# Projecting three units of the third batch's context between the ranking of the tokens and the first expert

## The chip, the cores and the metric

The kernel runs on one core of one Trainium2 chip. The metric is the device time of one launch in microseconds (us), of which a profiled execution also leaves a trace of every engine and DMA. Engines are named as in the profile: PE is TensorE (PEld its weight loads), DVE is VectorE, ACT is ScalarE, POOL is GpSimd and SP is SyncE, which here only issues DMAs. A lower time is better.

## The reference

Two layers act on x (8 batches, 100 tokens, 512 features) in fp32. Each layer has an attention and a mixture of eight experts, of which every token uses two.

```python
x = x + L0_xattn(layernorm(x), ctx, q_w, q_b, k_w, k_b, v_w, v_b, o_w, o_b)   # causal: only ctx[:, :100] counts
x = x + L0_ffn(layernorm(x), gamma, beta, Wg, bg, W1, b1, W2, b2)             # 8 experts, gelu, 2048 wide
x = x + L1_xattn(layernorm(x), ctx, ln_g, ln_b, Wq, Wkv, Wm, Wo, bo)          # keys: own 100 + projected ctx 722
x = x + L1_ffn(x, w_router, w_gate, w_up, w_down, ln_gamma, ln_beta)          # 8 experts, silu, 1024 wide

# the part of L1_xattn that the change is about: one projection serves as keys and as values
mem = split_heads(ctx @ Wm)          # (8, 722, 512) @ (512, 1024), 16 heads of 64
k = concatenate([k, mem]); v = concatenate([v, mem])
out = softmax(q k^T / 8) v
```

The expert part routes each token to the two experts with the largest router logits and adds the two answers by their normalized weights.

## The kernel before

**Stages.** The first attention runs over 32 units (4 groups of heads by 8 batches). Its output projection and the router follow, tile by tile over seven tiles of 128 tokens. When a group of tiles has its logits, `Route.group` (from L236) finds each token's two experts, ranks the tokens of each expert with two matmuls (L252, L253), and POOL sends the token rows into a table in DRAM, `sent`, by indirect DMA (L267). After the last group, `Route.order` sorts the experts by load, and each expert then fetches its rows (`arrived`, L344), transposes them into columns (L157, gain and shift on DVE at L164), computes its hidden layer (L680, Gelu on ACT at L684) and its products (L356). A second attention and a second expert part follow.

**Units of the second attention.** It runs over 64 units (b, ic): batch b, and a pair of heads ic of 8. A plain unit projects the context: for each of two halves of 361 columns, four matmuls (each of which the profile counts twice) and one eviction by ACT (L425, L429, `context_columns`); then six transposes and their evictions turn the result into values (L437 to L442, `context_rows`). Scores, softmax, transposes of the probabilities and the weighted sums follow.

**Kept units.** For the units in `EARLY` the projection is made before, by `project_early`, and stored in the DRAM tables `kept_keys` and `kept_values` (L457, L447). In the second attention such a unit loads both instead of computing them, and the first half of the next unit's projection is put beside it. Five units each of batches 0 and 1 are kept. Batch 0's are projected during the last units of the first attention and during the output projection, batch 1's between the first expert part and the second attention. Batches below `len(EARLY)` also spread the sums of their softmax by a POOL copy and a PE transpose (L792, L822), the others by three small DMAs through DRAM (L795, L797).

**The weights' ring.** `Weights` holds eight buffers of 1 MB. `load` takes the next pieces in a fixed order; a piece takes the buffer that comes free, and its DMA is issued on SP. Before, the eight first pieces are the four matrices of the first attention, two of `Wm`, and the two halves of batch 0's context; the experts' weights follow. The first two pieces of the first expert are loaded in `Route.order`, the next six when its first rows have arrived (a one-element POOL copy at L56 ties each to them).

**What sets the order.** The program is written in the order of the code, and a scheduler then places each engine's instructions; each engine's queue runs in that order. SP's queue holds at this place: the two fills of the DRAM tables with zeros, the stores of kept units, eight register loads of the experts' order (L297), and the weights.

Of the kernel before, what the change touches and what calls it, by code (L numbers as in the profile page):

```python
# [8 lines left out]
F32 = mybir.dt.float32  # L9
AF = mybir.ActivationFunctionType  # L10
ALU = mybir.AluOpType
AX = mybir.AxisListType

P = 128
D = 512
DC = D // P
B, T, S = 8, 100, 722
NT = B * T
HALF = NT // 2
NTILE = -(-NT // P)  # L20
# [10 lines left out]

EARLY = ((0, 1, 3, 5, 7), (0, 1, 3, 5, 7))
KEPT = {u: k for k, u in enumerate((b, ic) for b in range(len(EARLY)) for ic in EARLY[b])}

# [32 lines left out]
def two_layers(ctx: ExitStack, tc: tile.TileContext, a: dict, out: bass.AP):  # L67
# [9 lines left out]
    def context(b, h):  # L77
        return a["ctxT"][:, b, h * (S // 2) : (h + 1) * (S // 2)].rearrange("(c p) s -> p c s", p=P)

    pieces = [a[n] for n in ("k_w", "q_w", "v_w", "o_w")]  # L80
    W_EARLY = len(pieces)
    pieces += [a["Wm"][g] for g in range(2)] + [context(0, h) for h in range(2)]
    W_L0F = len(pieces)
    owner = [None, None]
# [120 lines left out]
    class Route:  # L205
# [29 lines left out]

        def group(self, i0, i1, xn):  # L236

# [10 lines left out]
            for i in range(i0, i1):  # L248
                nc.vector.tensor_tensor(self.before[:, i + 1, :], self.before[:, i, :], self.sel[:, i, :], ALU.add)
            ps = self.psum.tile([P, NTILE + 1, NE], F32, tag=self.tag, name=f"ps_rank{self.layer}")  # L250
            more = int(i1 == NTILE)
# [218 lines left out]
    with tc.tile_pool(name="a0", bufs=1) as ap, tc.tile_pool(name="a0w", bufs=3) as aw, tc.tile_pool(  # L470
# [24 lines left out]

        fill(sent)
        weights.load(W_L0F)
        fill(answers)

# [67 lines left out]
        for part in range(2):  # L567
            columns(0, part)
        units = [(c, b) for c in range(DC) for b in range(B)]
        prs, prTs = {}, {}  # L570
        steps = project_early(
            0, weights.tiles[W_EARLY + 2 : W_L0F], weights.tiles[W_EARLY : W_EARLY + 2], lambda: (
                fp.tile([P, S], F32, tag="nil", name="mT0", bufs=2), fp.tile([P, NSC, P], F32, tag="mv", name="mv0", bufs=2)
            ), ps, ("tp", "av"), lambda k: nc.sync.dma_start,
        )
        for n in range(len(units) + 2):
# [31 lines left out]
        def logits0(i):  # L608
            xT = xTf[:, :, i * P : i * P + rows[i]]
            to_columns(xT, xl[:, i, :], 0, rows[i], ps)  # L610
            router_logits(route.logits, i, xT, wg0, bg0, ps, "av")
            for i0, i1 in GROUPS[0]:
                if i1 == i + 1:
                    route.group(i0, i1, lambda i: xl[:, i, :])

# [17 lines left out]

        route.order(lambda: weights.load(W_L0F + 2))
        for _ in steps:
            pass
        where, more, (m1, m2) = route.where, route.more, route.m
# [433 lines left out]
```

## Time and profile before

| what | value |
|---|---|
| median of 3 runs | 1884.36 us (1884.31 to 1885.33) |
| the profiled execution | 1883.63 us, of it the span from first to last instruction 1882.0 us |
| mean granted PE clock | 0.959 |
| PE busy | 1725.5 us (92% of the span), 10414 matmuls |
| PEld busy | 1306.4 us |
| DVE, ACT, POOL busy | 594.9, 479.7, 147.8 us |
| DMA | 227.87 MB, mean 121 GB/s |
| all context projections (L425) | 1024 matmuls, 80 of them with the context in the weights' ring |

The span starts at the first instruction, and all places in time are counted from there. The page divides the span into 40 slices of 47 us and gives each engine's busy share in tenths. The timeline lists instructions in order with their start, duration and what ended the idle time before them; an answer by stretches gives busy time, granted clock and DMA share of chosen intervals. A busy PE is not always a PE at its peak, and a halved clock lengthens its matmuls.

### The profile page before, as it was taken

How to read it: one execution, taken by the hardware profiler on the slowest of the kernel's cores; microseconds unless marked ns; L12 is line 12 of the kernel's file. 1: busy time of each engine (PE TensorE's matmuls, PEld its weight loads, DVE VectorE, ACT ScalarE, POOL GpSimd, SP SyncE). 2: the span in 40 equal slices, each digit the busy share in tenths (PEclk: the TensorE clock that was granted, in tenths of full speed). 3: DMA queues.
4: the chain of work that ended last, by engine and by line, in shares of the span. 5: the costliest groups of instructions: out<-in, count | busy, mean ns of one | idle time of the engine just before them, and what ended most of it. 6: DMA issues, size and time to landing. Idle time of an engine off the chain costs nothing. (4 is left out here: it accounts for less than half of the span.)

```text
span 1882.0 us, 26422 instructions
## 1 busy us (share of the span) xinstructions
PE 1725.5 (92%) x10414; PEld 1306.4 (69%) x10414; DVE 594.9 (32%) x1462; ACT 479.7 (25%) x1400; POOL 147.8 (8%) x237
## 2 busy tenths in 40 slices
PE   5999689999999879999999999999999849999990
PEld 2455479999999645666666666666666528999990
DVE  4464510011111220454344424444444331111115
ACT  2364211111111132333333323333333210010110
POOL 4010310000000220000000000000000030000003
PEclk9999889999999989999999999999999969999995
DMA  9901374465555361131020300202201145555523
GB/s 367 414 28 56 124 284 169 182 222 189 203 201 219 108 235 45 40 96 56 5 37 5 59 3 5 37 6 37 27 6 15 6 159 221 192 185 200 207 79 114
DMA packets 74657, 227.87 MB, mean 121 GB/s; under 512 B 26273, under 2 KB 37161, under 8 KB 58129
## 3 DMA queue, kind: packets, MB, share of 16 engines
q1 hardware_dynamic: 53020, 177.98, 27.7%
q0 software_dynamic: 9888, 30.06, 5.1%
q10 hardware_dynamic: 11604, 17.95, 3.2%
q8 instruction: 86, 1.41, 0.3%
q14 instruction: 59, 0.48, 0.1%
HBM read 177.12 MB, written 48.83 MB: 120 GB/s over the span
## 5 line engine op out<-in xcount | busy, mean ns | idle before, releaser
L425 PE MATMUL ps_m<-cb,w 128*128 128x361 f32 x944 | 315.7, 486 | 0.0
L356 PE MATMUL ps_y<-h,w 128*128 128x256 f32 (+7 forms) x1536 | 280.5, 344 | 0.0
L356 PEld LDWEIGHTS ps_y<-h,w 128*128 128x128 f32 x1536 | 268.6, 190 | 7.9
L425 PEld LDWEIGHTS ps_m<-cb,w 128*128 128x128 f32 x944 | 180.5, 196 | 110.5 <-issue 18.0
L680 PE MATMUL ps_h<-xgT,w 128*128 128x256 f32 (+7 forms) x1024 | 189.5, 346 | 0.0
L680 PEld LDWEIGHTS ps_h<-xgT,w 128*128 128x128 f32 x1024 | 180.8, 192 | 5.8
L784 ACT ACTIVATE pr<-ps_sc,m 100x822 f32<-100x822 f32 x128 | 119.9, 942 | 175.7 <-issue 89.9
L808 DVE COPY prT<-ps_ptA 128x500 f32<-128x500 f32 x128 | 82.1, 678 | 187.1 <-PE ps_ptA L807 187.1
L782 DVE TENSOR_REDUCE m<-ps_sc 100x1 f32<-100x822 f32 x128 | 123.8, 1009 | 46.7 <-PE ps_sc L778 46.7
L684 ACT ACTIVATE h<-ps_h,s_b 128x256 f32<-128x256 f32 (+7 forms) x128 | 56.1, 438 | 303.8 <-PE ps_h L680 303.8
L429 ACT COPY mT<-ps_m 128x361 f32<-128x361 f32 x128 | 58.8, 460 | 251.5 <-PE ps_m L425 226.1
L414 PE MATMUL ps_col<-xT,w 128*128 128x400 f32 x320 | 115.1, 518 | 1.3 <-ACT xT L166 1.3
L950 PE MATMUL ps_g<-xgT,w 128*128 128x256 f32 (+7 forms) x512 | 104.3, 347 | 0.0
L950 PE MATMUL ps_u<-xgT,w 128*128 128x256 f32 (+7 forms) x512 | 102.8, 344 | 0.0
L414 PEld LDWEIGHTS ps_col<-xT,w 128*128 128x128 f32 x320 | 61.9, 197 | 47.3 <-issue 4.2
L950 PEld LDWEIGHTS ps_g<-xgT,w 128*128 128x128 f32 x512 | 91.4, 192 | 3.0
L950 PEld LDWEIGHTS ps_u<-xgT,w 128*128 128x128 f32 x512 | 90.7, 190 | 2.7
L778 PE MATMUL ps_sc<-mT,qT 64*100 64x311 f32 (+1 forms) x512 | 91.3, 468 | 0.0
L828 PEld LDWEIGHTS ps_av<-prT,mv 128*64 128x64 f32 (+1 forms) x1536 | 67.9, 137 | 31.3 <-issue 28.9
L955 ACT ACTIVATE sg<-ps_g 128x256 f32<-128x256 f32 (+7 forms) x64 | 22.3, 348 | 238.8 <-PE ps_g L950 238.8
L828 PE MATMUL ps_av<-prT,mv 128*64 128x100 f32 (+1 forms) x1536 | 80.6, 253 | 0.0
L807 PEld LDWEIGHTS ps_ptA<-ident,pr 100*128 100x128 f32 x640 | 65.2, 141 | 20.7 <-issue 10.6
(242 smaller groups left out, 1799.6 us busy)
## 6 DMA issues: line engine op xcount, KB each, us to landing
w<-in_W SPq DMA_DIRECT2D x64, 1024.0 KB
w<-in_w_gate SPq DMA_DIRECT2D x16, 1024.0 KB
w<-in_w_up SPq DMA_DIRECT2D x16, 1024.0 KB
w<-in_w_down SPq DMA_DIRECT2D x16, 1024.0 KB
sent<-nil SPq DMA_DIRECT2D x25, 512.0 KB
answers<-nil SPq DMA_DIRECT2D x25, 512.0 KB
cb<-in_ctxT ACTq DMA_DIRECT2D x16, 722.0 KB
xg<-sent POOLq DMA_DIRECT2D x18, 256.0 KB
```

The lines of the kernel that those rows point to most:

```text
L356: nc.tensor.matmul(py[:, k, :n], ws[f // 4][:, f % 4, dc * P : (dc + 1) * P], h[:, f, :n], start=f == 0, stop=f == nf - 1,)
L414: nc.tensor.matmul(ps[:, :HALF], w[c // 4][:, dc, (c % 4) * P : (c % 4 + 1) * P], xT[:, dc, cols], start=dc == 0, stop=dc == DC - 1,)
L425: nc.tensor.matmul(pm[:, : S // 2], w_m[ic // 4][:, dc, (ic % 4) * P : (ic % 4 + 1) * P], cb[h][:, dc, : S // 2], start=dc == 0, stop=dc = ...
L429: nc.scalar.copy(mT[:, h * (S // 2) : (h + 1) * (S // 2)], pm[:, : S // 2])
L680: nc.tensor.matmul(ph[:, :n], w[:, dc, j * P : (j + 1) * P], xg[:, dc, :n], start=dc == 0, stop=dc == DC - 1,)
L778: nc.tensor.matmul(sc[:, bank, c0:c1], qT[r, ic, q0 : q0 + T], keys_, start=True, stop=True)
L782: nc.vector.tensor_reduce(m, sc[:, :, :NKH], AX.XY, ALU.max, negate=True)
L784: nc.scalar.activation(pr.rearrange("p (a n) -> p a n", a=2), sc[:, :, :NKH], AF.Exp, bias=m, accum_out=sums[:, j : j + 1],)
L807: nc.tensor.transpose(pt[:, c, :], pr[:, T + c * P : T + (c + 1) * P], ident[:T, :T])
L808: nc.vector.tensor_copy(prT[:, : NSC - 1, :], pt)
L828: nc.tensor.matmul(po[r, 0, :], vj, prT[j][:w, c, :], start=c == 0, stop=c == NSC)
L950: nc.tensor.matmul(p_[:, :n], w_[:, dc, j * P : (j + 1) * P], xg[:, dc, :n], start=dc == 0, stop=dc == DC - 1,)
```

## The change

Three units of batch 2, with ic 1, 4 and 7, join the kept ones. Their context comes as two more pieces of the weights' ring, after the fill of the second DRAM table, in buffers that the first attention's matrices leave. Their projection is written after the ranking of the last group of tokens, before the first expert. To hold it there, `group` gets the two context tiles for its last call and adds to one element of each a zero that depends on the group's selection. With a third entry in `EARLY`, batch 2 spreads its softmax sums by the transpose.

```diff
-EARLY = ((0, 1, 3, 5, 7), (0, 1, 3, 5, 7))
+EARLY = ((0, 1, 3, 5, 7), (0, 1, 3, 5, 7), (1, 4, 7))
...
     pieces += [a["Wm"][g] for g in range(2)] + [context(0, h) for h in range(2)]
+    W_LATE = len(pieces)
+    pieces += [context(2, h) for h in range(2)]
     W_L0F = len(pieces)
...
-        def group(self, i0, i1, xn):
+        def group(self, i0, i1, xn, held=()):
...
+            for t in held:
+                nc.vector.scalar_tensor_tensor(
+                    t[:1, 0, :1], self.sel[:1, i1 - 1, :1], 0.0, t[:1, 0, :1], ALU.mult, ALU.add
+                )
             ps = self.psum.tile([P, NTILE + 1, NE], F32, tag=self.tag, name=f"ps_rank{self.layer}")
...
         fill(sent)
-        weights.load(W_L0F)
+        weights.load(W_LATE)
         fill(answers)
+        weights.load(W_L0F)
...
-        steps = project_early(
-            0, weights.tiles[W_EARLY + 2 : W_L0F], weights.tiles[W_EARLY : W_EARLY + 2], lambda: (
-                fp.tile([P, S], F32, tag="nil", name="mT0", bufs=2), fp.tile([P, NSC, P], F32, tag="mv", name="mv0", bufs=2)
-            ), ps, ("tp", "av"), lambda k: nc.sync.dma_start,
-        )
+        def kept_tiles():
+            mT = fp.tile([P, S], F32, tag="nil", name="mT0", bufs=2)
+            return mT, fp.tile([P, NSC, P], F32, tag="mv", name="mv0", bufs=2)
+
+        def by_sync(k):
+            return nc.sync.dma_start
+
+        early, late = weights.tiles[W_EARLY + 2 : W_LATE], weights.tiles[W_LATE:W_L0F]
+        steps = project_early(0, early, weights.tiles[W_EARLY : W_EARLY + 2], kept_tiles, ps, ("tp", "av"), by_sync)
...
-                    route.group(i0, i1, lambda i: xl[:, i, :])
+                    route.group(i0, i1, lambda i: xl[:, i, :], late if i1 == NTILE else ())
...
         route.order(lambda: weights.load(W_L0F + 2))
         for _ in steps:
             pass
+        for _ in project_early(2, late, weights.tiles[W_EARLY : W_EARLY + 2], kept_tiles, ps, ("tp", "av"), by_sync):
+            pass
```

More of the change, by code (lines that the diff above doesn't have):

```diff
@@ L496, in two_layers @@
         fill(sent)
+        weights.load(W_LATE)
+        fill(answers)
         weights.load(W_L0F)
-        fill(answers)
         xT = columns_tile("xT0")
```

## The prediction

> **What bounds the kernel now.** I read the page first. TensorE is busy for 92% of the span, so what matters is where it is not, and where its clock is low. The slices show two such places in the middle of the kernel; the change touches the first, slices 4 and 5 (188 to 282 us), and the long stretch from slice 16 on, the second attention.
>
> ```profile
> PE   5999689999999879999999999999999849999990
> PEclk9999889999999989999999999999999969999995
> ```
>
> Next the timeline of the first place, where the last group of rows is ranked, the rows are sent to DRAM and the first expert begins:
>
> ```profile
> 223.85 0.62 PE L252 MATMUL ps_rank<-before,every 128*128 128x24 f32 x2 [3.19 <-DVE sel L247]
> ...
> 236.78 1.18 POOL L344 DMA_DIRECT2D xg<-sent  x2 [5.39 <-issue]
> ...
> 239.83 1.94 PE L157 MATMUL ps_tp<-ident,xg 128*128 128x128 f32 x8 [14.94 <-DMA xg<-sent]
> ...
> 243.08 5.70 PE L680 MATMUL ps_h<-xgT,w 128*128 128x256 f32 x16
> 246.78 1.28 ACT L684 ACT_TABLE_LOAD   x1 [23.74 <-PE ps_h L680]
> ...
> 248.83 13.34 PE L680 MATMUL ps_h<-xgT,w 128*128 128x256 f32 x61
> ```
>
> TensorE does nothing for 14.94 us, between the last ranking matmul and the arrival of the expert's rows. The first two blocks of the expert's hidden layer then take 5.7 us. From the third on a block takes 1.73 us (the distance of its Gelus), so two take 3.46. The answer by stretches says why, with TensorE's busy time, the granted clock and the DMA share in each row:
>
> ```profile
> 219.98:223.39 3.41, 0.68 (x10) 0.50 0.42 161
> ...
> 240.46:243.87 3.41, 2.80 (x12) 0.50 0.82 280
> 243.87:247.29 3.42, 3.42 (x9) 0.50 0.89 335
> 247.29:250.70 3.41, 3.41 (x18) 1.00 1.05 381
> ```
>
> The clock is halved from 216.57 to 247.29 us. A stretch of 2.80 of 3.41 us busy didn't bring it back, a full one did; elsewhere 3.00 of 3.41 (646.65 to 650.06) did too.
>
> In the second attention TensorE never rests, so what leaves its queue there is worth its own time. By stretches of units (each ends at an exponential; columns us, then busy and count of PE and PEld):
>
> ```profile
> 822.10:888.80 66.70, 66.50 (x548) 44.22 (x546) 34.12 (x63) 26.47 (x81) 2.35 (x8) 1.00 0.20 62
> 1212.90:1283.30 70.40, 70.40 (x539) 48.19 (x534) 33.01 (x64) 26.45 (x78) 0.00 (x0) 1.00 0.11 10
> ```
>
> The first holds eight units of the second batch, four of them kept, and the value projection of the next batch; the other holds seven plain units, 10.06 us each.
>
> **What the skill says.** "TensorE: Matmul & The Clock Gate", Part 1, has the clock halved after an idle window of about 3.4 us and full after one busy window, the window free-running; the trace agrees in 3.41 us steps, though 929.95 to 933.37 was fully busy and the clock stayed halved one more. Part 4 says that transposes don't count as busy like matmuls; no stretch here separates that. "ScalarE: Activation LUTs", Table sets, has copies in every set, so the moved evictions need no table; the Gelu still does, 1.28 us here. "DMA: Bandwidth & Descriptors", Anatomy of one DMA, puts a DMA's semaphore wait on the issuing sequencer: a store that waits holds every weight load behind it on SP. The trace agrees: SP waited 11.7 us for one eviction at L442.
>
> **The change, part by part.** The built order of instructions, engine by engine, places the moved work; durations are from before.
>
> *Out of the second attention.* A plain unit spends on TensorE 16 projection matmuls (1044.33 to 1049.28, 4.95 us) and six transposes (1050.52 to 1051.32, 0.80 us): 5.75 us. All eight units of batch 2 also change how sums are spread, because b is now below the number of early batches: one more transpose each, 0.23 us (827.87 to 828.10), in place of three small DMAs. By counting, 3 x 5.75 - 8 x 0.23 = 15.4 us. By measured stretches: 66.7 less 6.8 for the projected values (a unit with it takes 16.8 instead of 10.0) is 59.9, against 8 x 10.06 = 80.5; four kept units saved 20.6 although eight had the transpose, so 5.6 each, and 3 x 5.6 - 1.8 = 15.0. The first batch gives 5.4 and 14.5. I take 14.9. Kept units 1, 4, 7 each have a plain neighbour to share its projection with, as there. The evictions that leave (VectorE 1.25 us a unit, ScalarE 0.92) were under TensorE's work, as are the nine loads that come instead (2.2 MB; DMA share is 0.11). Without that cover a load of 361 KB would cost about 1 us at the 373 to 418 GB/s of 249 to 262 us, three 3 us.
>
> *Into the first attention.* The third batch's context (1.44 MB) waits on SP for the value and query weights' last uses at 86.1 and 123.4 us, behind both fills. The next store on SP is at 143.6 us and DMA share is 0.01 there: nothing. If it were late it would hold VectorE, whose two new small operations (0.16 us each, the row of L142) wait for it; the margin is about 95 us.
>
> *Into the gap.* On TensorE the first moved matmul stands ahead of the last ranking pair. At half clock (2 x 0.31 x 2) it takes 1.2 us; with the two VectorE operations the rows are ranked, sent and fetched some 1.5 us later, 241.3 instead of 239.8. What stands behind it is what all Pool sends wait for, but it turns out covered, because the moved run ends later: 48 matmuls and 12 transposes in the open (14.85 + 1.6) and the ranking (0.5) are 17.0 us at full clock. It begins at 223.9 at half clock. If the stretch to 226.8 (85% busy, between 82% that failed and 88% that worked) brings the clock back, it has done 1.45 us of work by then and its last projection ends at 242.4; if the next does, at 244.1. The last unit has nothing to fill its eviction: two transposes wait for it (0.85 us), two more pairs follow, and the first expert's transposes use PSUM of the stage that ends, so they now wait for ScalarE's last three copies (0.91 us). Together 2.3 us: 244.7 or 246.4. Then to the first hidden matmul 2.9 us, as before with transposes at full speed: 247.6 or 249.3. In those 5 us TensorE is mostly idle, so I expect the clock to fall again and return at 250.7 or 254.1. Two blocks (3.46 us of work) and the table load between them put the third block at 253.1 to 255.2, where it was 248.83: 4.3 to 6.4 us. I take 5.5, and for the unknown clock 2 to 14.
>
> *The loads behind it.* Nine stores on SP stand ahead of the expert's weight pieces 3 to 8. The last waits for ScalarE's last copy, so those pieces start at about 247.5 instead of 239.95. Piece 3 is needed six blocks after the third, at about 264.5: 17 us for 1 MB, and all six (6.3 MB at those rates) take some 16. Nothing, but without this margin each us late would be one on the path. The stores add 2.1 MB while DMA share is 0.62. The third unit's tile waits for the first unit's store: SP's eight register loads end at 233.8 in the trace, so that store is issued near 235.3 and the tile is wanted near 240: nothing, at most 1 us.
>
> *Sum.* 1883.63 (span 1882.0 and 1.6 around it) - 14.9 + 5.5 = 1874.2. The median of the runs lies 0.73 above the profiled execution, so **1875.0**. 0.2% is 3.8 us, about what a measurement here can tell from no change.
>
> **Rivals.** (a) The gap takes the run free: the clock is back at once and stays, so that only 1.5 to 2 us of ranking are paid: 1871.2. For it: xg comes at 241.3, just before the run's end; against: the wait for ScalarE and the half clock at 220 to 226. (b) The weights' ring becomes the wait, piece 3 being late behind the stores. Its place is the ninth hidden block; it decides from a landing after 264.5; 5 us beyond that give 1880.0. Against: 17 us of slack. (c) Slower: the clock does not return during the run. 17.0 us of work then take 34, the run ends at 257.9, 14.7 us later than the middle of my cases: 1889.7. It loses once the clock returns after about 245.5. For it: the full stretch at 929.95 that didn't release; against: 243.87 and 646.65, which did at once. (d) The run isn't in the gap at all: the built order has it after the last logits and before the first expert's transposes, so this needs a late context, 1880 and up.
>
> **How the numbers follow.** The forecast, 1872 to 1879: 0.66. (a) 0.13, below 1872. (b), (d) and half-lasting clocks, 1879 to 1884: 0.12, of which two fifths are still faster by 3.8 us. (c) and beyond: 0.09. Faster 0.66 + 0.13 + 0.05 = 0.84, within 0.2% 0.08 (with what of (c) ends early), slower 0.08. The range 1869.5 to 1882.5 holds the forecast, nearly all of (a) and most of the third case.
>
> **What would show it.** L425's successor filling 224 to 243 with an idle gap before the first transposes of xg under 3 us and released by ScalarE, not by the DMA; the third hidden block at 253 to 255; a clock row of 0.50 near 247 to 254; batch 2's eight units near 87 us instead of 102; weight loads at 247. The forecast is wrong if the gap costs over 8 us (clock, or a hidden block released by a weight DMA), or if the kept units of batch 2 wait for their loads.

## The result, and the profile after

The changed kernel takes 1873.2 us (median of four runs, 1870.9 to 1874.0) against 1884.8 us before (four runs too): a ratio of 0.9941, with a 95% interval from 0.9929 to 0.9953, which is 8.9 to 13.4 us. The quotient of the two medians would be 0.9938. The forecast was 1875.0.

The two rows of the page that carried the first reading (busy tenths of TensorE and tenths of its granted clock, in 40 slices of the span) look like this after:

```profile
PE   5999899999999879999999999999999839999990
PEclk9999999999999989999999999999999969999995
```

The fourth and fifth digits of "9996899" have become "9998999": the hole behind the first attention is filled, and the clock's two eights of the same slices have become nines. Of all other digits only one of TensorE's has changed, from 4 to 3 near the end.

The timeline of that place, in the kernel after, with TensorE, the fetch on POOL, one copy on ScalarE and the first hidden blocks (start, duration, engine, line, what ended the idle time before it):

```profile
222.44 1.57 PE L432 MATMUL ps_m<-w,w 128*128 128x361 f32 x2 [3.11 <-DVE w L254]
223.81 0.46 PE L259 MATMUL ps_rank<-before,every 128*128 128x24 f32 x2
...
238.71 1.19 POOL L351 DMA_DIRECT2D xg<-sent  x2 [6.56 <-PE ps_m L432]
...
240.12 0.46 ACT L436 COPY mT<-ps_m 128x361 f32<-128x361 f32 x1 [2.69 <-DMA kept_keys<-mT]
...
241.45 0.66 PE L444 MATMUL ps_mv<-ident,mT 128*128 128x128 f32 x4 [0.33 <-ACT mT L436]
...
244.44 1.36 PE L159 MATMUL ps_tp<-ident,xg 128*128 128x128 f32 x8 [2.33 <-DMA xg<-sent]
...
247.43 4.97 PE L695 MATMUL ps_h<-xgT,w 128*128 128x256 f32 x16
...
252.58 9.76 PE L695 MATMUL ps_h<-xgT,w 128*128 128x256 f32 x44
```

(L432 and L444 are the projection and its transposes, L425 and L437 before; L259 the ranking; L351 the fetch; L695 the hidden layer. In the kernels of the experiments these numbers shift by up to four.) The run of the three late units fills 222.4 to 242.1 us. One moved matmul, which the profile counts twice, stands ahead of the last ranking pair. The fetch of the first expert's rows is issued at 238.7 instead of 236.8, and they are there at 244.4 instead of 239.8. The third hidden block starts at 252.58 instead of 248.83: in this execution the gap costs 3.75 us.

By stretches (columns: stretch, its length, then busy and count of PE, PEld, DVE, ACT and POOL, the granted clock, the DMA share, GB/s):

```profile
219.41:222.82 3.41, 0.38 (x1) 0.38 (x2) 3.00 (x24) 1.75 (x4) 2.19 (x3) 0.51 0.51 194
222.82:226.24 3.42, 3.42 (x9) 2.31 (x9) 2.10 (x21) 0.00 (x0) 0.43 (x1) 0.50 0.19 71
226.24:229.65 3.41, 3.41 (x12) 2.04 (x11) 3.38 (x11) 0.46 (x1) 3.10 (x2) 0.99 0.20 77
...
243.31:246.73 3.42, 1.38 (x9) 0.96 (x10) 1.56 (x5) 0.00 (x0) 1.08 (x7) 1.00 0.97 330
246.73:250.14 3.41, 3.41 (x11) 2.87 (x12) 2.35 (x8) 0.00 (x0) 0.82 (x2) 0.50 1.00 376
```

The clock comes back after the first full stretch, at 226.3 us, where before it came at 247.3. Then TensorE is busy for 1.38 of 3.42 us while it waits for the rows, and the next stretch, in which the first hidden blocks run, is at half clock again.

The third batch of the second attention, from its first exponential to that of the next batch, in the kernel before:

```profile
888.77:990.77 102.00, 99.73 (x664) 64.63 (x659) 41.39 (x82) 33.56 (x93) 0.00 (x0) 0.97 0.13 20
```

and after, with the two batches behind it:

```profile
890.28:976.72 86.44, 85.11 (x600) 54.99 (x596) 37.89 (x73) 30.90 (x86) 2.36 (x8) 0.96 0.13 40
976.72:1100.68 123.96, 121.70 (x732) 77.13 (x726) 44.94 (x103) 37.49 (x101) 3.94 (x4) 0.97 0.16 25
1100.68:1202.23 101.55, 99.34 (x658) 64.40 (x654) 41.60 (x82) 33.56 (x93) 0.00 (x0) 0.97 0.14 20
```

64 matmuls fewer by the profile's count, 15.6 us less. The next two batches take 1.9 and 1.4 us more than the 122.1 and 100.1 us that they took before; whether that is the change's doing is one of the questions below.

### The profile page after: what moved, and what is told of

Read it like the earlier page. It is cut to its first block, busy times and chain, and to the rows that moved or that the text cites. A ratio compares the mean times of both kernels' runs of the same rounds, so it can differ in the third digit from the quotient of the medians.

```text
span 1872.1 us, 26461 instructions
## 1 busy us (share of the span) xinstructions
PE 1730.2 (92%) x10422; PEld 1308.1 (70%) x10422; DVE 593.0 (32%) x1455; ACT 482.6 (26%) x1409; POOL 151.6 (8%) x245
## 5 line engine op out<-in xcount | busy, mean ns | idle before, releaser
L432 PE MATMUL ps_m<-cb,w 128*128 128x361 f32 x896 | 302.4, 489 | 0.0
L432 PEld LDWEIGHTS ps_m<-cb,w 128*128 128x128 f32 x896 | 172.0, 197 | 103.7 <-issue 16.9
L695 PE MATMUL ps_h<-xgT,w 128*128 128x256 f32 (+7 forms) x1024 | 188.8, 345 | 0.0
L695 PEld LDWEIGHTS ps_h<-xgT,w 128*128 128x128 f32 x1024 | 180.3, 191 | 5.7 <-ACT h L699 0.2
L823 DVE COPY prT<-ps_ptA 128x500 f32<-128x500 f32 x128 | 82.0, 678 | 178.2 <-PE ps_ptA L822 178.1
L793 PE MATMUL ps_sc<-mT,qT 64*100 64x411 f32 (+1 forms) x512 | 92.8, 468 | 0.0
```

The lines of the kernel that those rows point to most:

```text
L432: nc.tensor.matmul(pm[:, : S // 2], w_m[ic // 4][:, dc, (ic % 4) * P : (ic % 4 + 1) * P], cb[h][:, dc, : S // 2], start=dc == 0, stop=dc = ...
L695: nc.tensor.matmul(ph[:, :n], w[:, dc, j * P : (j + 1) * P], xg[:, dc, :n], start=dc == 0, stop=dc == DC - 1,)
L793: nc.tensor.matmul(sc[:, bank, c0:c1], qT[r, ic, q0 : q0 + T], keys_, start=True, stop=True)
L823: nc.vector.tensor_copy(prT[:, : NSC - 1, :], pt)
```

## The experiments

Three questions were open: what each half of the change is worth by itself, what makes the gap cost anything (the length of the run, the late ranking, the fetch, the clock), and whether the price can be lowered. Single executions of the kernel before differ by up to 11 us from each other on one chip (1876.6 to 1888.0), so a verdict needs the ratio with its interval, and a single profile shows a mechanism but not its mean size. The kernels ran on several chips, each beside the kernel before on the same chip; ratios from different chips are compared through that kernel alone.

This is what the gap looked like in each profiled execution, in us. "Clock back" is worked out from stretches of 0.4 us; "last ranking pair" is its start; "run ends" is the end of its last transposes; the "rows" column is the start of the first expert's transposes and what released the first four of them; the last column is where the third hidden block begins.

| kernel | clock back | last ranking pair | run ends | rows, released by | third hidden block |
|---|---|---|---|---|---|
| before | 247.3 | 223.9 | none | 239.8 fetch | 248.8 |
| attention alone | 248.2 | 224.5 | none | 241.1 fetch | 249.9 |
| changed | 226.3 | 223.8 | 242.1 | 244.4 fetch | 252.6 |
| changed, again | 228.7 | 223.2 | 243.0 | 243.9 ScalarE | 250.3 |
| gap alone | 230.4 | 225.3 | 244.9 | 245.7 ScalarE | 253.7 |
| no stores | 230.3 | 225.1 | 244.8 | 245.6 ScalarE | 252.0 |
| two units | 230.3 | 225.1 | 239.2 | 245.0 fetch | 253.4 |
| two, no stores | 229.8 | 224.7 | 238.8 | 241.9 fetch | 251.5 |
| four units | 228.8 | 223.6 | 249.3 | 250.2 ScalarE | 258.3 |
| early start | 227.1 | 227.2 | 244.4 | 247.5 fetch | 256.4 |
| early, four | 227.5 | 227.6 | 252.2 | 253.1 ScalarE | 259.5 |
| rank first | 230.6 | 224.1 | 245.4 | 246.2 ScalarE | 252.7 |
| two matmuls first | 230.1 | 223.8 | 243.8 | 244.6 ScalarE | 252.7 |
| sums by DMA | 227.9 | 222.9 | 242.5 | 243.3 ScalarE | 249.7 |

The attention alone leaves the gap as it was, and its third block is 1.1 us later than before: so much an execution can move it without any change there. Whatever the third block loses arrives whole at the end of the expert part. Its last Gelu, in the timelines of ScalarE before and after:

```profile
607.53 0.41 ACT L684 ACTIVATE h<-ps_h,s_b 128x176 f32<-128x176 f32 x1 [0.79 <-PE ps_h L680]
```

```profile
611.28 0.41 ACT L699 ACTIVATE h<-ps_h,s_b 128x176 f32<-128x176 f32 x1 [0.79 <-PE ps_h L695]
```

From the third block to this Gelu all fourteen executions take 358.6 to 358.8 us, at full clock. From there to the first exponential of the second attention they take 150.7 to 154.5 us, 152.7 before, 151.1 with the attention alone, 150.7 and 153.0 in two executions of the changed kernel: here up to 4 us come and go, 2.3 of them between two executions of one kernel.

In the second attention the batches can be compared by taking the time at half clock out: it comes in whole steps of 3.4 us, and each step lengthens its batch by 1.7. So counted, the third batch takes 98.6 us in the two kernels without kept units in it, 83.0 or 83.1 in the seven with three and sums by the transpose, 88.7 or 88.8 with two and 77.5 with four.

### The two halves apart

The gap alone: the late units are made and stored, and nobody reads them.

```diff
+READ = {u: k for u, k in KEPT.items() if u[0] < 2}
 ...
-            if (b, ic) in KEPT:
-                nc.sync.dma_start(out=mT, in_=kept_keys[KEPT[b, ic]])
+            if (b, ic) in READ:
+                nc.sync.dma_start(out=mT, in_=kept_keys[READ[b, ic]])
 ...
-            if b < len(EARLY):
+            if b < 2:
 ...
```

> The gap part alone: the three late units are projected and stored as in the changed kernel, but the second attention doesn't use them and runs as before (their stored context is computed and never read). Theory (the gap costs what the trace shows, and part of it is won back later): third hidden block of the first expert at 252 to 253 us instead of 248.8, the first exponential of the second attention 1.5 to 4 us later than before, the whole 1.5 to 4 us slower than before (ratio 1.0008 to 1.0021). Rival (my prediction's term, 5.5 us, all carried to the end): 5 to 6 us slower, ratio 1.0027 to 1.0032. Second rival (the slower batches 3 and 4 of the changed kernel come with the shift in time and not with the kept units): the shift and 3 us more, 5 to 7 us slower, with batch 3 at 124 us.

The attention alone, made from the kernel before:

```diff
+KEPT.update({(2, 1): KEPT[1, 1], (2, 4): KEPT[1, 3], (2, 7): KEPT[1, 7]})
 ...
-            if b < len(EARLY):
+            if b < 3:
 ...
```

> The attention part alone: nothing is projected late; units 1, 4 and 7 of the third batch load the context kept for units 1, 3 and 7 of the second batch, so their values are another batch's, and the work is that of three kept units. Theory (three times 5.6 less eight transposes, 14.9): batch 3 of the trace's eight (the third) at 86 to 88 us instead of 102.0, and 14 to 16 us faster than before, ratio 0.9915 to 0.9926. Rival (the 3.3 us that the two batches behind it lose in the changed kernel come from the kept units themselves): 11 to 12.5 us faster, ratio 0.9934 to 0.9942. If both parts add up, the gap-alone kernel and this one together give the changed kernel's 11.6 us.

Measured: the gap alone gives a ratio of 1.0024 (1.0016 to 1.0032), 4.5 us slower, between 3.0 and 6.0. The attention alone gives 0.9922 (0.9908 to 0.9937), 14.7 us faster, between 11.9 and 17.3. Together 0.9946, beside the changed kernel's 0.9941: the two parts add up within their intervals, and no third effect is needed.

In the profile of the gap alone (timeline of TensorE) it is ScalarE that releases the first four of the first expert's transposes; the next eight wait 0.9 us more for the fetch, and the third block is 4.8 us later than before:

```profile
245.72 0.66 PE L160 MATMUL ps_tp<-ident,xg 128*128 128x128 f32 x4 [0.83 <-ACT mv L450]
247.25 1.86 PE L160 MATMUL ps_tp<-ident,xg 128*128 128x128 f32 x8 [0.87 <-DMA xg<-sent]
...
253.66 8.69 PE L696 MATMUL ps_h<-xgT,w 128*128 128x256 f32 x39
```

Its second attention begins at 765.8 us instead of 760.2, 5.6 us later, so here nothing was won back on the way. My guess beforehand that the gap's price shrinks later, drawn from the changed kernel's first profile (first exponential at 762.0), was not borne out. The interval holds its upper part as well as the 5.5 us of the prediction; the profile, of an execution 2.4 us slower than this kernel's median, shows the latter. What the first profile won back lies behind the last Gelu, in the stretch that differs by 2.3 us between two executions of the changed kernel.

The second rival of the gap alone falls: its batch behind the third takes 122.1 us, as before, though everything is shifted. In the attention-alone profile the same batch takes 124.0; the whole is 14.7 us faster, and only the edge of its interval, 11.9, reaches the 11 to 12.5 of the rival there. The clock settles it: the two batches each held one step at half clock before (3.4 us) and two in the changed kernel's first profile (6.8), and with that taken out they take 120.3 and 98.4 us before, 120.6 and 98.1 after. In the no-stores and the rank-first profiles below, which have the same three kept units, they held one step each again and took 122.3 and 100.1. So the 3.3 us are steps of the clock and no work of the kept units. Why the first of the two batches held a second step in nine of twelve profiles with kept units, and in neither of the two without, is not shown.

### The changed kernel once more

> The changed kernel once more, beside the other runs of this call. Theory (what the gap costs depends on where the clock's 3.41 us steps fall: the profile of the changed kernel had the clock back at 226.3 us, the three other kernels with a late run had it back one step later, at about 230): the time is 0.993 to 0.9955 of before, and this profile shows either the first transposes of the expert's rows at 244.4 released by the fetch, with the second attention's first exponential near 762, or at 246 to 247 with a wait for ScalarE's last copy, and that exponential at 764 to 767. Rival (the profile of the changed kernel is what always happens, and the 4.5 us of the gap-alone kernel come from elsewhere): transposes at 244 to 244.8 and the exponential at 761 to 763.

Measured: 0.9936 (0.9919 to 0.9954). The profile (TensorE's timeline) is neither of the two pictures:

```profile
243.86 0.66 PE L159 MATMUL ps_tp<-ident,xg 128*128 128x128 f32 x4 [0.83 <-ACT mv L449]
244.83 0.66 PE L159 MATMUL ps_tp<-ident,xg 128*128 128x128 f32 x4 [0.32 <-DMA xg<-sent]
...
250.32 11.92 PE L695 MATMUL ps_h<-xgT,w 128*128 128x256 f32 x54
```

The first four transposes wait for ScalarE's last copy, the next four for the fetch: run and fetch end about a microsecond apart. The clock came back 2.4 us later than in the first profile (228.7), and the third block is nevertheless 2.3 us earlier (250.3), because here the clock did not fall a second time. The one picture wasn't always the case, then, but the step I had offered in its place (transposes at 246 to 247, the attention at 764 or later) wasn't seen in this kernel either; its attention began at 762.0. "TensorE: Matmul & The Clock Gate" of the Trainium skill, Part 1, says that the window over which the clock is decided is free-running and that the same kernel therefore starts with a varying number of matmuls at the low clock. The two profiles of one kernel agree: the clock was back at 226.3 and 228.7 us. In the third batch it shows as well: 83.1 us here, with no halved stretch near 926 us, and 86.4 in the first profile, which was halved from 926.0 to 932.8. The same stretch in the second profile (the granted clock is the third number from the end):

```profile
890.27:973.42 83.15, 81.82 (x600) 53.00 (x596) 37.89 (x73) 30.95 (x87) 2.38 (x8) 1.00 0.14 41
```

### How many units

One size was changed: `(1, 3, 5, 7)`, and then `(1, 4)`, in the place of `(1, 4, 7)`.

```diff
-EARLY = ((0, 1, 3, 5, 7), (0, 1, 3, 5, 7), (1, 4, 7))
+EARLY = ((0, 1, 3, 5, 7), (0, 1, 3, 5, 7), (1, 3, 5, 7))
```

> One size changed: four late units of the third batch (1, 3, 5, 7) instead of three. Theory (the run ended 2.3 us before the rows came, so a fourth unit is 2.3 us cheaper than its 5.75 us of TensorE work): third hidden block 3.0 to 4.3 us later than with three, at 255.6 to 256.9 us, the third batch's units 5.6 us shorter than with three, whole 1 to 2.6 us faster than the changed kernel, ratio to before 0.9927 to 0.9936. Rival (the fourth unit's tiles wait for the second unit's stores on SP, or the expert's weight pieces, now issued at 251 or later, become the wait): third or a later hidden block 6 us or more later than with three, whole the same as the changed kernel or up to 3 us slower, ratio 0.994 to 0.996.

> One size changed: two late units (1 and 4) instead of three. Theory (the rows can't come before 241 us, so the first two units are nearly free and the third costs what it lengthens the run): third batch at 91 to 93 us (102.0 less 2 x 5.6 and plus 8 x 0.23), third hidden block at 249 to 251 us, 0 to 2 us later than before; whole 7 to 9.5 us faster than before, ratio 0.995 to 0.9963. Rival (the gap's price is in the late ranking, in the clock and the stores, not in the run's length): third hidden block at 251.5 to 253 as with three units, whole 5 to 6.5 us faster, ratio 0.9966 to 0.9974.

Measured: four units 0.9949 (0.9931 to 0.9967), two units 0.9972 (0.9959 to 0.9985), three 0.9941 and 0.9936. In us against before that is 9.6 faster with four, 11.1 to 12.1 with three, 5.3 with two.

With two units the run ends 5.7 us before the rows come, and the third block is as late as with three (timeline of TensorE, two units):

```profile
244.96 1.09 PE L159 MATMUL ps_tp<-ident,xg 128*128 128x128 f32 x4 [5.73 <-DMA xg<-sent]
...
253.41 8.90 PE L695 MATMUL ps_h<-xgT,w 128*128 128x256 f32 x40
```

So the rival held and my theory for two units fell: the gap's price is not in the run's length as long as that stays below what fits, and the third unit, which adds 5.75 us of TensorE work, is nearly free. (The third batch took 88.8 us, less than the 91 to 93 that I gave; it was never at half clock in this execution, as in the second profile of the changed kernel with 83.1. At equal clock the third unit takes 5.7 us off the batch.)

The fourth unit isn't free. The third block is at 258.3, 4.6 us behind the gap-alone profile and 5.7 behind the first changed one; in return the third batch falls to 79.2 us from 86.4. The two cancel, and the whole is the same within its interval: the rival's numbers. Neither of its two mechanisms is in the trace, though. ScalarE waits 1.6 us for a store (2.7 and 1.6 in the two profiles with three units), no hidden block waits for a weight, and TensorE goes from the third unit to the fourth without a gap. The run simply ends last, at 249.3, where theory had put it. What theory had wrong is the slack: 2.3 us in the first profile, but in this execution, with the clock back at 228.8, the rows were there at 243.0 and the third unit's last copy ended at 244.0, so that no slack was left.

### The stores

The late stores left out: nine with three units, six with two. The second attention then reads what the second batch kept.

```diff
 ...
-            store(out=kept_keys[KEPT[b, ic]], in_=mT)
+            if b < 2:
+                store(out=kept_keys[KEPT[b, ic]], in_=mT)
 ...
-            moved(store, mv, kept_values[KEPT[b, ic]], True)
+            if b < 2:
+                moved(store, mv, kept_values[KEPT[b, ic]], True)
 ...
```

> The changed kernel with the nine stores of the late units left out (the second attention loads the context kept for the second batch in their place, so those units' values are another batch's). Theory (the late stores lengthen the fetch of the first expert's rows, 5.6 us from issue to landing instead of 3.0): the fetch lands within 3 to 4 us, the first transposes of the rows start 1.2 to 2 us earlier than 244.4, at 242.4 to 243.2 (not before the last eviction of the run at 242.9, if that is what waits next), third hidden block near 251, whole 1 to 2 us faster than the changed kernel: ratio to before 0.9930 to 0.9936. Rival (the fetch is late because the ranking, the sends and the expert's first two weight pieces are, whatever the stores do): first transposes at 244 to 244.8, ratio to before 0.9938 to 0.9946, as the changed kernel.

> Two late units (1 and 4) and their stores left out (the second attention loads what was kept for the second batch, so those units' values are another batch's). With two units the fetch of the rows releases the first expert's transposes, so the stores should tell here. Theory (the stores beside it lengthen the fetch by 2 us): fetch lands within 3 to 3.5 us of its issue, transposes at 242 to 243.5 instead of 244.96, third hidden block at 250 to 252 instead of 253.4, ratio to before 0.0006 to 0.0015 below the two-unit kernel's 0.9972. Rival (the late ranking alone makes the rows late): transposes at 244.5 or later, third hidden block at 253 or later, ratio 0.9966 to 0.9978.

Measured: with three units 0.9936 (0.9920 to 0.9953), not to be told from the changed kernel, with two 0.9959 (0.9946 to 0.9973) where it was 0.9972 with stores. In the traces the fetch of the rows takes 3.0 us from its issue to the first use of its data without stores (238.84 to 241.82 with two units, 239.86 to 242.84 with three), as before (236.78 to 239.75), and 4.6 to 6.5 us with them (238.28 to 243.10 in the second profile of the changed kernel, 238.71 to 244.36 in the first, 240.91 to 247.37 with the early start). With three units that gains nothing, since the run then ends at 244.8 and ScalarE's copy is the wait. With two, where the fetch decides, the transposes come 3 us earlier:

```profile
241.90 1.26 PE L161 MATMUL ps_tp<-ident,xg 128*128 128x128 f32 x8 [3.12 <-DMA xg<-sent]
...
251.52 10.75 PE L699 MATMUL ps_h<-xgT,w 128*128 128x256 f32 x49
```

Of these 3.1 us (244.96 to 241.90), 1.8 are the fetch itself and 1.2 its earlier issue, of which 0.8 is a shorter wait of POOL behind its last send (5.8 instead of 6.7 us); why that wait is shorter is not shown. The third block gains 1.9 of the 3.1; the rest goes to the clock, which comes back at 250.3 here and at 250.8 with the stores: the two blocks that begin sooner (245.5 instead of 248.5) spend more of their time at half of it and take 6.0 us instead of 4.8. That the stores lengthen the fetch is shown by the traces; that it is worth anything in the whole is not certain, for the two intervals overlap.

### The start of the run and the ranking

Four kernels moved the point until which the late units are held back. The early start ties them to the last logits:

```diff
 ...
             g, v = i1 - i0, self.logits[:, i0:i1, :]
+            for t in held:
+                nc.vector.scalar_tensor_tensor(
+                    t[:1, 0, :1], v[:1, g - 1, :1], 0.0, t[:1, 0, :1], ALU.mult, ALU.add
+                )
 ...
-            for t in held:
-                nc.vector.scalar_tensor_tensor(
-                    t[:1, 0, :1], self.sel[:1, i1 - 1, :1], 0.0, t[:1, 0, :1], ALU.mult, ALU.add
-                )
```

> One part changed: the late units are held back only until the last logits, not until the last selection, so the moved run may fill the 3.1 us in which TensorE waits for VectorE before the ranking; five of its matmuls (ten as the profile counts them) then stand ahead of the last ranking pair instead of one. Theory (the late, slow start of the run is what makes it end after the rows): the run begins at 219.5 to 221 us instead of 222.4 to 223.9, ends by 239 to 242.5, third hidden block at 249.5 to 252.5, 1 to 3.5 us faster than the changed kernel: ratio to before 0.9922 to 0.9936. Rival (with the clock halved there, ten matmuls take 6.2 us, the ranking and the sends come 2 us later, and the fetch of the rows becomes the wait): last ranking pair after 225.5, first transposes of the rows at 245 to 247, the whole as the changed kernel.

Measured: 0.9969 (0.9962 to 0.9977), half of the gain gone. The rival held, and its price was larger than I had given it. The timeline of the early start:

```profile
221.16 6.20 PE L432 MATMUL ps_m<-w,w 128*128 128x361 f32 x10 [0.44 <-DVE w L243]
...
227.20 0.30 PE L259 MATMUL ps_rank<-before,every 128*128 128x24 f32 x2
...
240.91 1.18 POOL L351 DMA_DIRECT2D xg<-sent  x2 [5.84 <-PE ps_m L432]
...
247.46 1.94 PE L159 MATMUL ps_tp<-ident,xg 128*128 128x128 f32 x8 [3.10 <-DMA xg<-sent]
...
256.44 5.88 PE L695 MATMUL ps_h<-xgT,w 128*128 128x256 f32 x26
```

Five matmuls, ten in the profile's count, take 6.2 us at half clock, all of them ahead of the ranking pair, which comes at 227.2 instead of 223.8. Everything that hangs on it follows: the fetch is issued at 240.9 and lands at 247.4. TensorE starts its run 1.3 us earlier than in the first profile of the changed kernel, and the expert's third block comes 4 us later than there. What stands ahead of the ranking is on the path; how soon the run begins is not. (The profiled execution was 3.7 us slower than this kernel's median.) The run itself was also held up: its last transposes stood 2.6 us for a copy of ScalarE, which had waited 5.6 us for the store of an earlier unit. With three units the rows came later still, so that this cost nothing.

The same with four units:

> Early start and four late units (1, 3, 5, 7) together. Theory (the earlier start makes room for part of the fourth unit): third batch at 79 us as with four units before, third hidden block at 254 to 256.5 instead of 258, whole 2 to 5 us faster than four units with the late start: ratio to before 0.992 to 0.994, at or below the changed kernel. Rival (the fourth unit's 5.75 us always end after the rows, whatever the start): third hidden block at 257 or later, ratio 0.9945 to 0.9955.

Measured: 0.9950 (0.9933 to 0.9967), third block at 259.5, the run again the last to end. The rival held in the whole: starting early gains a fourth unit nothing. But the trace shows a wait here that the late start does not have. The earlier run reaches its third unit before the store of the first is done, so that ScalarE and then TensorE stand for it:

```profile
243.09 0.82 ACT L436 COPY mT<-ps_m 128x361 f32<-128x361 f32 x2 [5.49 <-DMA kept_keys<-mT]
...
243.60 0.44 PE L444 MATMUL ps_mv<-ident,mT 128*128 128x128 f32 x2 [2.53 <-ACT mT L436]
```

Behind it the clock is halved from 244.6 to 248.0, and the run ends at 252.2 instead of 249.3. What an early start would be worth to four units without this wait is not shown.

Rank first ties the late units to the last ranking (`row`, written from the ranking's result, in the place of `self.sel`), so that nothing stands ahead of it:

```diff
-            for t in held:
 ...
             nc.vector.tensor_tensor(row, ps[:, :g, :], base.unsqueeze(1).to_broadcast([P, g, NE]), ALU.add)
+            for t in held:
+                nc.vector.scalar_tensor_tensor(
+                    t[:1, 0, :1], row[:1, g - 1, :1], 0.0, t[:1, 0, :1], ALU.mult, ALU.add
+                )
```

> One part changed: the late units are held back until the last ranking is done, so no moved matmul stands ahead of the ranking pair. Theory (in most executions the end of the run and ScalarE's last copy release the expert's first transposes, not the fetch): ranking pair 1.2 to 1.5 us earlier, run begins 1 us or so later than in the changed kernel, transposes and third hidden block the same to 1 us later, ratio to before that of the changed kernel or up to 0.0006 above. Rival (the fetch of the rows decides, as in the first profile of the changed kernel): third hidden block 1 to 1.5 us earlier, ratio 0.0006 to 0.0008 below.

Measured: 0.9955 (0.9940 to 0.9971), which overlaps with the changed kernel's and lies on its slow side. The profile: the ranking pair stands directly behind its wait, and the run begins 1.5 us after it, at 225.6, ends at 245.4, and ScalarE's copy releases the transposes:

```profile
224.11 0.62 PE L255 MATMUL ps_rank<-before,every 128*128 128x24 f32 x2 [3.19 <-DVE before L252]
...
225.59 7.57 PE L432 MATMUL ps_m<-w,w 128*128 128x361 f32 x16 [0.45 <-DVE w L260]
...
246.23 1.09 PE L159 MATMUL ps_tp<-ident,xg 128*128 128x128 f32 x8 [0.83 <-ACT mv L449]
```

That is the theory's picture, and the rival's 1 to 1.5 us of gain are excluded by the interval. The ranking itself came at 224.1, no sooner on the clock than in the changed kernel, as the halved stretch began at 216.9 here and slowed the last logits; the 1.4 us are seen only against the end of the wait.

The last of the four lets just two matmuls go after the last logits and holds the rest until the ranking is done:

```diff
 ...
-                    route.group(i0, i1, lambda i: xl[:, i, :], late if i1 == NTILE else ())
+                    route.group(i0, i1, lambda i: xl[:, i, :], ([late[0][:1, 0, :1]], [late[0][:1, 2, :1], late[1][:1, 0, :1]]) if i1 == NTILE else ((), ()))
```

(`held[0]` is tied to the last logits, `held[1]` to `row`, by the same small operation.)

> One part changed: only the first two matmuls of the moved run (four as the profile counts them, 2.5 us at half clock) may start after the last logits, so that they fill the 3.1 us in which TensorE waits for VectorE; the rest is held back until the last ranking is done, so nothing that is late stands ahead of the ranking pair. Theory (two things make the gap dear: the idle 3.1 us before the run, and what stands ahead of the ranking): ranking pair at 222.3 to 224.3 us, as in the kernel before, run 1 to 2.5 us ahead of the rank-first kernel's, clock back at or before 229, third hidden block at 249.5 to 251.5 where the changed kernel's two profiles had 252.6 and 250.3; whole 0 to 2.5 us faster than the changed kernel, ratio to before 0.9925 to 0.9938. Rival (the fetch of the rows beside the stores is the wait as soon as the run is short enough): transposes at 243.5 to 245 released by the fetch, third hidden block at 251 to 252.6, ratio as the changed kernel, 0.9936 to 0.9945.

Measured: 0.9963 (0.9950 to 0.9977), outside of both expectations and slower than the changed kernel's 0.9941 and 0.9936, though its interval just touches theirs. In the trace the two matmuls fit where they were meant to, from 220.93 to 223.7, and the ranking follows at 223.75; but the clock was back only at 230.1, the run ended at 243.8, and the third block came at 252.7, which is that of the changed kernel's first profile. The filled 3.1 us bought nothing. Why the whole is 4 to 5 us slower than the changed kernel isn't explained: the profiled execution shows at most 2.4 us of it at the third block (1.6 of them because the first two blocks ran partly at half clock, 5.2 us instead of 3.6) and 1.6 at the start of the second attention (763.6), each against the second profile of the changed kernel. The second timing of the changed kernel was on another chip. I leave that open.

### The sums of the third batch

One part was undone: the condition, in three places, that gives the third batch the extra transposes.

```diff
-            if b < len(EARLY):
+            if b < 2:
 ...
```

> One part undone: the third batch's units spread their softmax sums by three small DMAs, as before, and not by a transpose; all else is the changed kernel. Theory (the eight transposes cost TensorE 0.23 us each and the DMAs nothing): third batch 1.8 us shorter, 84 to 85 us where the changed kernel had 86.4 (81 to 81.5 where it had 83.1), whole 1 to 2.5 us faster than the changed kernel, ratio to before 0.9925 to 0.9933. Rival (the small DMAs stand on SP behind the loads of kept units, which wait for buffers, so that TensorE or VectorE wait for the sums): third batch at 86 us or more, ratio 0.9938 to 0.996.

Measured: 0.9999 (0.9989 to 1.0009). The whole gain of the change is gone. The rival held, and by far more than its numbers. In the timeline of this kernel, SP's DMAs (marked SPq), VectorE and TensorE:

```profile
890.50 0.31 SPq L810 DMA_DIRECT2D shares<-sums  x1
897.52 1.16 SPq L812 DMA_DIRECT2D over<-shares  x2
...
905.74 0.26 DVE L850 TENSOR_TENSOR qT<-qT,over 128x100 f32<-128x100 f32 x1 [8.27 <-DMA over<-shares]
...
906.64 0.69 PE L444 MATMUL ps_mv<-ident,mT 128*128 128x128 f32 x2 [6.76 <-DVE prT L823]
```

The sums of the first unit leave at 890.5; the way to DRAM and back takes until 905.7, 15.2 us. In a stretch of plain units (1216.2 to 1226.4 in this profile) it takes 10.2, and VectorE then waits 0.3 us for it, because a plain unit is 10 us long. Here the unit before was shorter, 7 us, and the trip itself 5 us longer. VectorE stands at the multiplication for 8.3 us, the evictions of the transposed softmax weights (L823) queue behind it, and TensorE stops for 6.8; behind that the clock is halved from 903.8 to 910.6. The third batch takes 90.6 us, 87.2 at full clock where it was 83.1: 4.1 us of waiting and 3.4 of half clock. Against the 86.4 and 83.1 us of the changed kernel that accounts for 4 to 7.5 of the 11 us. The rest is open; the profiled execution is the fastest of this kernel's fourteen, and whether the others stall more no trace here shows. The rival's detail was another: the sums left as soon as they were computed, with no load waiting ahead of them; the small DMAs themselves are slow. Nor does it take kept units: in the kernel before, one such trip took 17.1 us (965.7 to 982.8), and VectorE waited 6.7 us for it, but TensorE had 12 us of projections to do and did not stop. So what a short unit takes away is the cover; why some trips are so long is not shown.

No version beat the changed kernel.

## Why the prediction was right, step by step

**Out of the second attention: 14.9 us.** The half by itself measured 14.7 (11.9 to 17.3); the batch fell to 86.4, where "near 87" stood. Both ways of counting held; at equal clock the batch lost 15.5 us, close to the 15.4 of the first. The eight transposes were costed at 1.8 us against "three small DMAs" at nothing. The sum was right, but the comparison was not thought through: without the transposes the DMAs would have cost the whole gain. That they are part of a kept unit's price, and not a loss beside it, is seen only in the last experiment.

**The early load: nothing.** The changed kernel ranks the group before the last at 215.0 us, where the kernel before does it at 214.9, and at 214.4 in its second profile. (That its run begins at 222.4, where the ranking began at 223.9, is the clock's doing: it was halved at 219.4 instead of 216.6.)

**The gap: 5.5 us (4.3 to 6.4).** The gap alone measured 4.5 (3.0 to 6.0), its third hidden block came 4.8 us later. The size was a little too large, within the stated ends. That it came out so near is in part luck, because two of its terms were off in opposite directions: the run ended sooner than given, and the rows came later. Of its terms:

- The end of the last projection, 242.4 or, if the clock takes one step more, 244.1: it came at 240.9, 241.8, 241.2 and 243.7 in the four profiles of this gap (the changed kernel twice, sums by DMA, the gap alone). The reason given, the stretch in which the clock comes back, was right. In the first profile it came back after the first step and in the other three after one more. But all four were earlier than their case, by 0.4 to 2.9 us, mostly because in three of them the run began at 221.5 to 222.4 us and not at 223.9.
- "1.5 us later, 241.3" for the rows: wrong. They came at 242.2 to 245.3, between 2.4 and 5.5 us after those of before. The mis-sized term is the fetch, which I left at its 3.0 us although "the stores add 2.1 MB while DMA share is 0.62" stood in the text; it measured 4.6 to 5.6 in these four, and 3.0 with the stores left out. I had priced the stores only for the weights.
- "Released by ScalarE, not by the DMA": wrong in the first profile, where the fetch ended the wait at 244.4, and half right in the other three, where ScalarE released the first four transposes and the fetch the next, after a further wait of 0.3 to 0.9 us. The two ends lie so close that the execution decides. The idle gap of 2.33 us is below the 3 us given.
- The clock "to fall again and return at 250.7 or 254.1": it returned at 250.2 in the first profile and near 251 in the gap alone, and did not fall in the second profile nor with the sums by DMA. The third block at 253.1 to 255.2 was 253.7, 252.6, 250.3 and 249.7: so the forecast described the dear case as the only one. Where the clock fell, the first two blocks took 4.6 and 5.0 us; where it did not, 3.6.

**The loads behind it: nothing.** The six weight pieces started at 244.6, 3 us sooner than I had them, and no hidden block waited for a weight in the gap. Rival (b) needed a landing after 264.5; that no later block waited is seen from the 358.7 us between the third block and the last Gelu, the same as before. The third unit's tile waited 2.69 us on ScalarE for the first unit's store, not "at most 1". TensorE lost nothing to it, for its 0.33 us behind that copy stand in the kernel without stores too: a wrong wait at the right price, though not a safe one, as the early start with its 2.6 us shows.

**The rivals.** (a), the free gap at 1871.2: the second profile of the changed kernel, with a third block at 250.3, is that case (1.5 us at the third block), but the gap alone, at least 3.0 us slower than before, excludes it as the mean. (c): the clock was back between 226.3 and 230.6 in every kernel with a late run, and had to stay away until about 245.5. (d): the run was in the gap.

The result, 1873.2, lies 1.8 below the forecast: by the halves measured apart, 1.0 of it would be the gap's 4.5 for 5.5, and what is left is below the spread of the runs.

## What to carry to other kernels

Work moved into an idle stretch is free up to the later of the ends that were there already, here the arrival of data, and costs full price beyond; but the stretch is seldom untouched by it, so price again the DMA that ends the stretch, with the new transfers beside it, and count what is placed ahead of the instruction that this DMA hangs on, at the clock of that place. Making a stage's units shorter shortens the cover of everything that ran beside them: a round trip through DRAM of 10 us or more that was hidden under units of 10 us is not under units of 7. Where two ends meet within a microsecond, forecast both. And before a difference of a few microseconds between two profiles is explained by work, take out the time at half clock in each.

## What the runs showed of the hardware that I had not expected

- The clock's steps fall differently in two executions of one kernel, and an earlier return is not always the better one: back at 226.3, the third block came at 252.6; back at 228.7, at 250.3, because in the first the next step was mostly idle (1.38 of 3.42 us busy) and the two hidden blocks behind it ran at half clock, while the second held 1.97 us in its idlest step and kept the clock. In this gap, over all twelve profiles with a late run, the clock fell after steps with at most 1.7 us busy and stayed after those with 1.75 or more; ahead of the gap, among small matmuls and transposes, it fell after 1.9 to 2.6 us too.
- At half clock, the first step that the run took up brought the clock back in one of the twelve profiles, after 3.41 of 3.41 us busy. In the other eleven it did not, after 2.6 to 3.4 us, once with the step full; each time the next full step did.
- The time at half clock comes in steps of 3.4 us, and one step more or less makes a batch of the second attention 1.7 us longer or shorter (122.1 and 124.0, or 86.4 and 83.1 with two).
- Filling 2.8 of the 3.1 idle us before the run did not bring the clock back sooner (230.1 us, and 230.4 with the gap alone, where it had been halved at the same place).
- A fetch of 256 KB pieces took 3.0 us in the four kernels without stores beside it and 4.6 to 6.5 in the ten profiles with them, though the stores are issued by SP and the fetch by POOL.
- A DMA of 0.8 KB with 200 separate values (the sums) let its follower start 6 to 9 us after its issue (1216.18 to 1222.18, 890.50 to 897.52, 959.92 to 969.00, all in the kernel with the sums by DMA).
